# Layer 1: the bias folding moved to later steps one matrix at a time, and the last images' expert sums shared by three engines

## The chip, the cores and the metric

The kernel runs on one core of one Trainium2 chip. The metric is the device time of one launch in microseconds (us), as the median of several runs. Engines are named as in the profile: PE is TensorE (PEld its weight loads), DVE is VectorE, ACT is ScalarE, POOL is GpSimd, SP issues DMAs.

## What is computed

The input is `x` of shape (4, 32, 128, 128). Layer 0 is a spectral (FFT) convolution with attention between images; it writes its result `x1` to memory. Layer 1, where the change is, sees `x1` as four sequences of 4096 tokens with 128 channels. Cut to what matters here:

```python
# layer 1
t = x1 as tokens                                  # (4, 4096, 128)
# causal additive attention on normalised tokens
z = ln(t)
f, g = z @ W1[:128], z @ W1[128:]                 # 16 features each
score[i, j] = sum_a w2[a] * tanh(f[i, a] + g[j, a] + b1[a]) + b2
e = exp(score) * (j < i)
t = t + (e / (e.sum(-1) + 1e-10)) @ z
# mixture of 8 experts, the best two of each token
z = ln(t)
p, i = top_2(softmax(z @ router_w + router_b));  p = p / p.sum(-1)
t = t + sum_k p[k] * (z @ expert_w[i[k]] + expert_b[i[k]])
```

## The kernel before

A block of 128 tokens is called an image. Eight images make a chunk (16 chunks in all), and half a chunk, 512 query columns, is worked on at a time. **A unit** is one half of a chunk against one block of 128 keys; there are 528 units (`units`). The tanh sum is written with exponentials, so that it becomes matrix products: for each unit PE makes denominators `d` and numerators `n` (three groups each, L1869).

The order of the work in layer 1 is written out by hand, inside `tc.manual_schedule()`: a loop over `u`, in which each pass (a **step**) issues one stage of several units.

- PE: `d` of unit u together with `n` of unit u-1 (`products`, L1869).
- ACT: the logarithm of `d` of unit u into `r` (L1938), and then the exponential of minus that (L1950).
- DVE: `r = n * r` of unit u-1, in two instructions (L1943). POOL: two adds of the three groups into `e` (L1946, L1947).
- ACT: the exponential of `e` of unit u-2 (L1954); POOL multiplies the causal mask in on the diagonal (L1959).
- PE: the sum of `e` times the normalised keys of unit u-4 into `po` (`attend`, L1888); when a half is complete DVE copies it out (L1898).

Behind these each step issues **pieces** of the remaining work from queues: for the next chunk its load, its normalisation (statistics on DVE, L1504 and L1508; application on POOL, L1518), its transposes (L1533, L1534), its keys and queries (`as_keys`, `as_queries`: one matmul `pz`, one ACT exponential L1572 or L1587, and DMAs that copy 64 rows to the other half of the partitions); and for a chunk whose attention is complete the pieces of `finish`. A piece carries a kind and two costs, for DVE and POOL. The rule in the loop is: at most one piece with PE work in a step (`kind and pe`), at most 1.8 us of DVE cost and, beyond the first, 0.9 us of POOL cost. Whatever does not fit waits for the next step. A chunk's keys and queries are hurried when its first unit comes near (`hurry`).

All pieces with PE work use one PSUM bank, `"m"` (`misc`), until the loop is over; then four more banks join it. [...] a piece's matmul whose bank is still being read by DVE holds up the `d` and `n` of the next step.

`finish` adds the attention to the tokens `xc`, normalises (`x2`), transposes (`x2t`), computes router logits `pl` and the best two experts with DVE (`first`, `second`), the weights on ACT and POOL (`share`, `weights`, L1757), and then the experts (`experts`, L1770 and L1779): n products (image k, expert e) at a time, 2 to 4 by `share_of(u)`. PE writes them to one bank `px`, and DVE adds each, times its weight, to its image:

```python
nc.vector.scalar_tensor_tensor(
    xc[:, k], px[:, i], wgt[:, k, e : e + 1], xc[:, k], ALU.mult, ALU.add
)
```

After the loop, the remaining queues are emptied, and the last half chunk (four images, 32 products in 8 groups of 4) is finished alone with `last=True`; its store on SP is the last DMA of the kernel.

`biases` folds the router's and the experts' biases into the matrices `wr` (128x8) and `we` (128x1024), so that the kernel needs no separate addition: for each of three parts one matmul with `mean` (L1678), one DVE subtraction (L1679) and one DVE instruction that adds the bias row, read from `par` or `eb` (L1680). It is called at step u == 4, outside the rule for pieces, for all three parts. The tile `eb` lies in the buffer that `x2` uses from the first `finish` on.

Of the kernel before, what the change touches and what calls it, by code (L numbers as in the profile page):

```python
# [7 lines left out]
F32 = mybir.dt.float32  # L8
AF = mybir.ActivationFunctionType
ALU = mybir.AluOpType  # L10
# [3 lines left out]
P = 128  # L14
B, T, H, C = 4, 32, 128, 128
# [9 lines left out]
NE = 8  # L25
IC = 1024
NB = IC // P
QC = 512
# [4 lines left out]
B1, W2, RB = 11, 27, 43  # L33
# [1396 lines left out]
def layer1(tc, x1, w1t_in, signs, vec17, expert_w, expert_b, router_w, small_row, out):  # L1430


    nc = tc.nc
# [7 lines left out]
    def misc(name):  # L1441
        if not pools:
            return before.tile([P, 512], F32, name=name, tag="wide")
        banks.append(banks.pop(0))
        return ps.tile([P, 512], F32, name=name, tag=banks[-1])
# [14 lines left out]
    for s, dst in ((0, mq), (1, mk)):  # L1460
        pm = misc("pm")
# [21 lines left out]


    NONE, SOME, KEEPS, KEPT, EXPERTS, LATER = range(6)

    gap = (LATER, 0.0, 0.0, lambda: None)

# [142 lines left out]
    const, other_keys, work, small, ps = (p.__enter__() for p in pools)  # L1631
    banks.append("m")
    tc.keep_in_program_order(nc.scalar.preload_act_table_set("natural_log_exp_and_others"))
    par = const.tile([P, NSMALL], F32, name="par1")
    nc.sync.dma_start(out=par, in_=small_row.partition_broadcast(P))
    wr = const.tile([P, NE], F32, name="wr")
    nc.sync.dma_start(out=wr, in_=router_w)
    we = const.tile([P, NE, C], F32, name="we")
# [24 lines left out]
    mean = const.tile([P, P], F32, name="mean")  # L1663
    nc.vector.memset(mean, 1.0 / C)
    eb = work.tile([P, NE, C], F32, name="eb", tag="x2", bufs=1)
# [1 line left out]
        out=eb.rearrange("p e c -> p (e c)"),  # L1667
        in_=expert_b.rearrange("e c -> (e c)").partition_broadcast(P),
    )
    def biases():  # L1670
        for w, row in (
            (wr, par[:, RB : RB + NE]),
            (we[:, :4].rearrange("p e c -> p (e c)"), eb[:, :4].rearrange("p e c -> p (e c)")),
            (we[:, 4:].rearrange("p e c -> p (e c)"), eb[:, 4:].rearrange("p e c -> p (e c)")),
        ):
            n = w.shape[1]
            pm = misc("pm")[:, :n]
            nc.tensor.matmul(pm, mean, w, start=True, stop=True)  # L1678
            nc.vector.tensor_tensor(w, w, pm, ALU.subtract)  # L1679
            nc.vector.scalar_tensor_tensor(w, row, 1.0 / C, w, ALU.mult, ALU.add)  # L1680

    def finish(b, i0, nb, att, last=False):


        fe = [P, nb, NE]

        def over_e(t):
            return t.unsqueeze(2).to_broadcast(fe)

        def stat(tag):  # L1690
            return small.tile([P, NB], F32, name=tag, tag=tag)[:, :nb]

        xc = work.tile([P, NB, C], F32, name="xc", tag="xc", bufs=4)
        nc.sync.dma_start(out=xc[:, :nb], in_=x1[b, i0 : i0 + nb].rearrange("t w c -> w t c"))


        def attention(k0, n):
            pa = misc("pa")[:, : n * (C + 1)].rearrange("p (k c) -> p k c", c=C + 1)
            for k in range(n):
                q = (k0 + k) % QB * P  # L1700
                nc.tensor.matmul(  # L1701
                    pa[:, k], att[(k0 + k) // QB][:, q : q + P], centre, start=True, stop=True
                )
            rden = small.tile([P, 3, 1], F32, name="rden", tag="rden")[:, :n]
            nc.vector.tensor_scalar(rden, pa[:, :, C:], 1e-10, None, ALU.add)
            nc.vector.reciprocal(rden, rden)
            for k in range(n):
                nc.vector.scalar_tensor_tensor(
                    xc[:, k0 + k], pa[:, k, :C], rden[:, k], xc[:, k0 + k], ALU.mult, ALU.add
                )  # L1710

        x2 = work.tile([P, NB, C], F32, name="x2", tag="x2", bufs=1)
        x2t = work.tile([P, IC], F32, name="x2t", **(dict(tag="r", bufs=3) if last else dict(tag="x2t")))
        hot1, hot2, wgt = (
            small.tile([P, NB, NE], F32, name=n, tag=n, bufs=3)[:, :nb] for n in ("hot1", "hot2", "wgt")
        )
        top1, top2, vm, w1 = (stat(n) for n in ("top1", "top2", "vm", "w1"))

        at = {}

        def greatest(top, hot):
            pl, v = at["pl"], at["v"]
            nc.vector.tensor_reduce(top, pl, AX.X, ALU.max)
            nc.vector.tensor_tensor(v, pl, over_e(top), ALU.is_equal)
            nc.vector.tensor_tensor(v, v, rank.unsqueeze(1).to_broadcast(fe), ALU.mult)
            nc.vector.tensor_reduce(vm, v, AX.X, ALU.max)
            nc.vector.tensor_tensor(hot, v, over_e(vm), ALU.is_equal)

        def first():
            bank = misc("pl")
            at["pl"], at["v"] = (
                bank[:, i * nb * NE : (i + 1) * nb * NE].rearrange("p (k e) -> p k e", e=NE)
                for i in range(2)
            )
            pl = at["pl"]
            for k in range(nb):
                nc.tensor.matmul(pl[:, k], x2t[:, k * P : (k + 1) * P], wr, start=True, stop=True)  # L1739
            greatest(top1, hot1)  # L1740
            nc.vector.scalar_tensor_tensor(pl, hot1, -1e30, pl, ALU.mult, ALU.add)

        def second():
            greatest(top2, hot2)
            nc.gpsimd.tensor_tensor(top2, top2, top1, ALU.subtract)

        def share():

            nc.scalar.activation(top2, top2, AF.Exp)
            nc.scalar.activation(w1, top2, AF.Ln, bias=one)  # L1750
            nc.scalar.activation(w1, w1, AF.Exp, scale=-1.0)

        def weights():
            nc.gpsimd.tensor_tensor(top2, top2, w1, ALU.mult)
            nc.gpsimd.tensor_tensor(hot1, hot1, over_e(w1), ALU.mult)
            nc.gpsimd.tensor_tensor(hot2, hot2, over_e(top2), ALU.mult)
            nc.gpsimd.tensor_tensor(wgt, hot1, hot2, ALU.add)  # L1757

        products = [(k, e) for k in range(nb) for e in range(NE)]

        def experts(n):

            now = products[:n]
            del products[:n]
            px = misc("px").rearrange("p (e c) -> p e c", c=C)
            at_e = 0
            for k in sorted({k for k, _ in now}):
                own = [e for of, e in now if of == k]
                m = len(own)
                nc.tensor.matmul(  # L1770
                    px[:, at_e : at_e + m],
                    x2t[:, k * P : (k + 1) * P],
                    we[:, own[0] : own[0] + m],
                    start=True,
                    stop=True,
                )
                at_e += m
            for i, (k, e) in enumerate(now):
                nc.vector.scalar_tensor_tensor(  # L1779
                    xc[:, k], px[:, i], wgt[:, k, e : e + 1], xc[:, k], ALU.mult, ALU.add  # L1780
                )
            if not products:
                nc.sync.dma_start(
                    out=out[b, i0 : i0 + nb].rearrange("t w c -> w t c"), in_=xc[:, :nb]
                )
            return len(products)

        pieces = [(NONE, 0.0, 0.0, lambda: None), gap] * 2
        sums, after = norm_pieces(xc, x2, nb)
        step = 3 if nb == NB else 2  # L1790
        for k in range(0, nb, step):
            n = min(step, nb - k)
            pieces.append((SOME, 0.4 + 0.3 * n, 0.0, lambda k=k, n=n: attention(k, n)))
            pieces += sums[k // 2 : (k + n) // 2]
        pieces += after
        pieces += [
            (SOME, 0.7, 0.0, lambda h=h: transpose_half(x2, x2t, h)) for h in range(nb // 4)
        ]
        pieces += [(KEEPS, 1.4, 0.0, first), (KEPT, 1.2, 0.2, second), gap]
        pieces += [(NONE, 0.0, 0.0, share), gap, (NONE, 0.0, 1.1, weights), gap]  # L1800
        pieces.append((EXPERTS, nb * NE, 0.0, experts))
        return pieces

# [108 lines left out]
    def share_of(u):  # L1912

        queued = sum(ended, []) + todo
        left = sum(p[1] for p in queued if p[0] == EXPERTS) + sum(NE * p[2] for p in ending)
        others = sum(p[0] in (SOME, KEEPS) for p in queued) + NB * len(ending)
        until = min([f + 20 * (f < first_unit[-1]) for f in first_unit if f > u] + [len(units)])
        return min(max(-(-left // max(until - u - others, 1)), 2), 4)
# [12 lines left out]
    with tc.manual_schedule():  # L1931
        for u in range(len(units) + 4):
# [18 lines left out]
            if 0 <= u - 2 < len(units):  # L1951
                c, h, _, parts = units[u - 2]
                e = live[u - 2, "e"]
# [12 lines left out]
                elif is_last and h == 1:  # L1966
                    ending.append((*chunks[c], NB, [sums[c, h] for h in range(2)]))

            if u == 4:
                biases()  # L1970
            if unopened and not norm and u >= opens[unopened[0]]:
                norm_of = unopened.pop(0)
                norm, *opened[norm_of] = begin(norm_of)
# [12 lines left out]
            queues = sorted(ended, key=lambda p: len(p) <= 1)  # L1986
            queues = hurry + queues + [q for q in (todo, norm) if q not in hurry]
            pe, dve, pool = False, 0.0, 0.0
            n = share_of(u)
            for pieces in queues:  # L1990
                while pieces:
# [123 lines left out]
```

## Time and profile before

| what | value |
|---|---|
| median of 3 runs | 2872.17 us (2871.64 to 2875.78) |
| profiled execution, own time | 2870.23 us |
| profiled execution, span | 2868.6 us |
| granted TensorE clock, mean | 0.985 |
| busy share of the span | PE 95%, ACT 81%, DVE 76%, POOL 71% |
| layer 1's units | from 836.6 us to 2797.4 us of the span (first and last start of L1950) |
| work after the last unit | 2797.4 us to the end at 2868.6 us |

The profile is one execution. Busy time is what an engine executed; waiting for a semaphore is not busy. A row of the timeline gives the start, the duration of the (merged) instructions, the engine, the line, the operation with its output and inputs and shapes, the count, and in square brackets how long the engine was idle before it and what released it. L1950 is issued once for each unit, so the distance of two starts of L1950 is the time of a unit.

### The profile page before, as it was taken

The numbers are of one execution on the slowest core, as the hardware profiler recorded it, in microseconds if no ns is written. First come the engines' busy times: TensorE is split into PE (matmuls) and PEld (weight loads), VectorE is DVE, ScalarE is ACT, GpSimd is POOL, SyncE is SP. The second block draws the span as 40 slices with busy tenths as digits, with TensorE's granted clock in tenths as the row PEclk, the third lists the DMA queues.
The fourth block names the chain that finished last, engine by engine and source line by source line (L and its number), as shares of the span: only waits on it lengthen the run. The fifth ranks groups of instructions, "written<-read, shape, count | busy, mean of one in ns | idle before, by whom it ended". The sixth has DMA issues, their size and how long they took to land.

```text
span 2868.6 us, 52910 instructions
## 1 busy us (share of the span) xinstructions
PE 2720.7 (95%) x19638; PEld 1379.6 (48%) x19638; DVE 2175.5 (76%) x4830; ACT 2315.7 (81%) x3243; POOL 2035.3 (71%) x1804
## 2 busy tenths in 40 slices
PE   8898999988879999999999999999999999999996
PEld 5565664654644444445444444544444454444442
DVE  5888788778766677777787776778788677877777
ACT  3555466465459999999999999999999999999990
POOL 2706418137028998998998988898898888878872
PEclk9999999999989999999999999999999999999998
DMA  4403204114030101002101000110100010010000
GB/s 103 125 1 106 88 8 149 39 42 138 3 81 23 41 1 41 8 14 47 40 2 34 16 16 19 41 27 23 41 1 16 20 34 19 16 34 1 16 12 19
DMA packets 151153, 107.72 MB, mean 38 GB/s; under 512 B 36302, under 2 KB 140017, under 8 KB 150897
## 3 DMA queue, kind: packets, MB, share of 16 engines
q1 hardware_dynamic: 147633, 102.26, 13.5%
q8 instruction: 155, 2.54, 0.4%
q10 hardware_dynamic: 3264, 2.10, 0.3%
q14 instruction: 101, 0.83, 0.1%
HBM read 63.86 MB, written 19.50 MB: 29 GB/s over the span
## 4 chain that ended last, share of the span: by engine, by line
PE 60%; ACT 7%; DVE 5%; POOL 3%; issue 2%; DMA 0%; SPq 0%; DVEq 0%; POOLq 0%; ACTq 0%
PE d L1869 26%; PE po L1888 15%; PE px L1770 6%; PE n L1869 5%; ACT r L1938 3%; DVE r L1943 1%; ACT e L1954 1%; DVE xc L1779 1%; ACT r L1950 1%; PE pl L1739 1%; POOL e L1946 1%; PE pz L1571 1%; PE pa L1701 1%; PE pt L1533 1%; PE pz L1586 1%
## 5 line engine op out<-in xcount | busy, mean ns | idle before, releaser
L1943 DVE TENSOR_TENSOR r<-n,r 128x1024 f32<-128x1024 f32 (+1 forms) x1056 | 961.9, 953 | 457.3 <-PE n L1869 327.9
L1938 ACT ACTIVATE r<-d 128x1024 f32<-128x1024 f32 (+1 forms) x1056 | 793.6, 803 | 63.6 <-PE n L1869 51.4
L1946 POOL TENSOR_TENSOR e<-r 128x512 f32<-128x512 f32 x528 | 673.4, 1275 | 213.0 <-DVE r L1943 211.4
L1950 ACT ACTIVATE r<-r 128x1536 f32<-128x1536 f32 x528 | 783.6, 1484 | 16.8
L1947 POOL TENSOR_TENSOR e<-e,r 128x512 f32<-128x512 f32 x528 | 671.8, 1272 | 41.4
L1869 PE MATMUL d<-qe,ke 32*128 32x512 f32 (+3 forms) x2304 | 604.5, 601 | 16.9 <-ACT r L1938 12.8
L1869 PE MATMUL n<-qe,ke 32*128 32x512 f32 (+3 forms) x2304 | 604.6, 601 | 0.0
L1888 PE MATMUL po<-e,kx 128*128 128x512 f32 (+3 forms) x1152 | 594.4, 605 | 3.0 <-POOL e L1959 3.0
L1869 PE MATMUL n<-qf,kf 32*128 32x512 f32 (+3 forms) x2304 | 550.8, 553 | 0.0
L1869 PE MATMUL d<-qf,kf 32*128 32x512 f32 (+3 forms) x2304 | 549.1, 552 | 0.0
L1779 DVE SCALAR_TENSOR_TENSOR xc<-px,wgt,xc 128x128 f32<-128x128 f32 x1024 | 354.5, 349 | 34.9 <-PE px L1770 5.2
L1888 PEld LDWEIGHTS po<-e,kx 128*128 128x128 f32 x1152 | 175.4, 188 | 376.1 <-issue 297.6
L1954 ACT ACTIVATE e<-e 128x512 f32<-128x512 f32 x528 | 324.2, 614 | 14.7 <-POOL e L1947 14.7
L1869 PEld LDWEIGHTS d<-qe,ke 32*128 32x128 f32 x2304 | 176.5, 183 | 302.0 <-ACT r L1938 273.2
L1869 PEld LDWEIGHTS d<-qf,kf 32*128 32x128 f32 x2304 | 219.1, 185 | 164.4 <-issue 152.6
L1770 PE MATMUL px<-we,x2t 128*128 128x512 f32 (+3 forms) x644 | 271.0, 515 | 5.7 <-DVE xc L1779 2.0
L989 POOL TENSOR_TENSOR u<-xb,gb 128x858 f32<-128x858 f32 (+1 forms) x112 | 220.6, 2008 | 42.4 <-PE po L926 37.6
L1869 PEld LDWEIGHTS n<-qf,kf 32*128 32x128 f32 x2304 | 227.5, 185 | 24.8 <-issue 17.2
L1140 POOL TENSOR_TENSOR spec<-part,part 128x512 f32<-128x512 f32 x16 | 25.7, 1609 | 284.8 <-DVE gn_r_t L253 93.0
L993 DVE TENSOR_TENSOR u<-xw,gb 128x858 f32<-128x858 f32 (+1 forms) x208 | 215.6, 1105 | 6.7 <-ACT xw L980 3.1
L1770 PEld LDWEIGHTS px<-we,x2t 128*128 128x128 f32 x644 | 119.3, 193 | 140.4 <-issue 116.8
L1869 PEld LDWEIGHTS n<-qe,ke 32*128 32x128 f32 x2304 | 176.8, 183 | 10.9 <-DVE r L1943 1.5
(425 smaller groups left out, 3409.3 us busy)
## 6 DMA issues: line engine op xcount, KB each, us to landing
xb<-xd SPq DMA_DIRECT2D x128, 214.5 KB
xc<-x SPq DMA_DIRECT2D x29, 512.0 KB
x<-x SPq DMA_DIRECT2D x16, 512.0 KB
qf<-qe SPq DMA_DIRECT2D x64, 128.0 KB
out<-xc SPq DMA_DIRECT2D x15, 512.0 KB
x<-in_x SPq DMA_DIRECT2D x14, 512.0 KB
xb<-xd SPq DMA_DIRECT2D x32, 198.0 KB
kf<-ke SPq DMA_DIRECT2D x32, 128.0 KB
```

The source lines that it names most:

```text
L989: weighed = nc.gpsimd.tensor_tensor(u, xb, gk, ALU.mult)
L993: weighed_last = nc.vector.tensor_tensor(u, xw, gk, ALU.mult)
L1770: nc.tensor.matmul(px[:, at_e : at_e + m], x2t[:, k * P : (k + 1) * P], we[:, own[0] : own[0] + m], start=True, stop=True,)
L1779: nc.vector.scalar_tensor_tensor(xc[:, k], px[:, i], wgt[:, k, e : e + 1], xc[:, k], ALU.mult, ALU.add)
L1869: nc.tensor.matmul(o, k, q, start=turn == 0 or g > 0, stop=turn == 1 or g > 0)
L1888: nc.tensor.matmul(sums[c, h][:, q0 : q0 + c1 - c0], kx[:, jb], e[:, c0:c1], start=jb == 0, stop=is_last and q0 > 2 * P, skip_group_check= ...
L1938: nc.scalar.activation(r[:, g], d, AF.Ln, scale=1.0 / DSCALE)
L1943: nc.vector.tensor_tensor(r[:, g], part, r[:, g], ALU.mult)
L1946: nc.gpsimd.tensor_tensor(e, r[:, 1], r[:, 2], ALU.add)
L1947: nc.gpsimd.tensor_tensor(e, e, r[:, 0], ALU.add)
L1950: nc.scalar.activation(r, r, AF.Exp, scale=-1.0)
L1954: nc.scalar.activation(e, e, AF.Exp)
```

## The change

Three things are edited.

1. `biases()` at step 4 is gone. The three parts stand in a list, and each even step from u = 10 (`BIASES`) takes one: first `wr`, then `we[:, :4]` at u = 12, then `we[:, 4:]` at u = 14. Such a step counts as having its PE piece, and 1.4 us of DVE cost, so that the pieces that would have stood there move on.
2. In the last `finish` the products are reordered: four experts of one image, then the same four of the next image, so that groups of even and odd images alternate.
3. In the last `finish` the groups of odd images are no longer added by DVE: ACT copies each product from PSUM to a tile `scaled` times its weight, and POOL adds it to `xc`.

```diff
+    BIASES = 10
...
-    def biases():
-        for w, row in (
-            (wr, par[:, RB : RB + NE]),
-            (we[:, :4].rearrange("p e c -> p (e c)"), eb[:, :4].rearrange("p e c -> p (e c)")),
-            (we[:, 4:].rearrange("p e c -> p (e c)"), eb[:, 4:].rearrange("p e c -> p (e c)")),
-        ):
-            n = w.shape[1]
-            pm = misc("pm")[:, :n]
-            nc.tensor.matmul(pm, mean, w, start=True, stop=True)
-            nc.vector.tensor_tensor(w, w, pm, ALU.subtract)
-            nc.vector.scalar_tensor_tensor(w, row, 1.0 / C, w, ALU.mult, ALU.add)
+    def bias(w, row):
+
+        n = w.shape[1]
+        pm = misc("pm")[:, :n]
+        nc.tensor.matmul(pm, mean, w, start=True, stop=True)
+        nc.vector.tensor_tensor(w, w, pm, ALU.subtract)
+        nc.vector.scalar_tensor_tensor(w, row, 1.0 / C, w, ALU.mult, ALU.add)
+
+    biases = [
+        (we[:, 4:].rearrange("p e c -> p (e c)"), eb[:, 4:].rearrange("p e c -> p (e c)")),
+        (we[:, :4].rearrange("p e c -> p (e c)"), eb[:, :4].rearrange("p e c -> p (e c)")),
+        (wr, par[:, RB : RB + NE]),
+    ]
...
         products = [(k, e) for k in range(nb) for e in range(NE)]
+        if last:
+            products = [(k + i, e + j) for k in range(0, nb, 2) for e in (0, 4) for i in range(2) for j in range(4)]
...
+            if last and now[0][0] % 2:
+                scaled = work.tile([P, QC], F32, name="scaled", tag="e", bufs=5)
+                scaled = scaled.rearrange("p (e c) -> p e c", c=C)
+                for i, (k, e) in enumerate(now):
+                    nc.scalar.activation(scaled[:, i], px[:, i], AF.Copy, scale=wgt[:, k, e : e + 1])
+                    nc.gpsimd.tensor_tensor(xc[:, k], xc[:, k], scaled[:, i], ALU.add)
+                now = []
             for i, (k, e) in enumerate(now):
                 nc.vector.scalar_tensor_tensor(
...
-            if u == 4:
-                biases()
...
             pe, dve, pool = False, 0.0, 0.0
+            if biases and u >= BIASES and u % 2 == 0:
+                bias(*biases.pop())
+                pe, dve = True, 1.4
             n = share_of(u)
```

## The prediction

> **What bounds the kernel now.** I read the page's busy line first. It spreads its shares over two layers, so it does not tell what an edit in layer 1 is worth:
>
> ```profile
> PE 2720.7 (95%) x19638; PEld 1379.6 (48%) x19638; DVE 2175.5 (76%) x4830; ACT 2315.7 (81%) x3243; POOL 2035.3 (71%) x1804
> ```
>
> So I went to the timeline of layer 1 by ACT alone. L1950 runs once in a unit, and the distance of its starts is the unit's time:
>
> ```profile
> 851.01 1.48 ACT L1950 ACTIVATE r<-r 128x1536 f32<-128x1536 f32 x1
> 852.40 0.61 ACT L1954 ACTIVATE e<-e 128x512 f32<-128x512 f32 x1
> 857.36 0.69 ACT L1572 ACTIVATE ke<-pz,off 128x512 f32<-128x512 f32 x1 [4.35 <-PE pz L1571]
> 860.59 1.51 ACT L1938 ACTIVATE r<-d 128x1024 f32<-128x1024 f32 x2 [2.54 <-PE n L1869]
> 862.14 1.48 ACT L1950 ACTIVATE r<-r 128x1536 f32<-128x1536 f32 x1
> ...
> 866.15 1.48 ACT L1950 ACTIVATE r<-r 128x1536 f32<-128x1536 f32 x1
> ...
> 869.58 1.48 ACT L1950 ACTIVATE r<-r 128x1536 f32<-128x1536 f32 x1
> ...
> 873.01 1.48 ACT L1950 ACTIVATE r<-r 128x1536 f32<-128x1536 f32 x1
> ```
>
> The last two distances are 3.43 us with no idle time in brackets: ACT runs back to back and sets the pace. From 862.14 to 866.15 it is 4.01 us, because a key or query exponential (0.67 us) joins. One unit, from 851.01 to 862.14, takes **11.13 us**, and ACT sits idle 4.35 + 2.54 us in it. I took all 528 starts and sorted the units by the experts piece in the step before (median; units with a key or query exponential apart): no PE piece 3.43 us, two products 3.44, three 3.63, four 3.84. With three or four PE, not ACT, is the bound.
>
> The slow unit is where `biases()` stands. In the timeline of all engines:
>
> ```profile
> 850.76 1.27 POOL L1946 TENSOR_TENSOR e<-r 128x512 f32<-128x512 f32 x1
> 850.81 1.24 DVE L1680 SCALAR_TENSOR_TENSOR wr<-par,wr 128x8 f32<-128x8 f32 x1
> 850.83 1.12 PE L1678 MATMUL pm<-we,mean 128*128 128x512 f32 x2 [0.81 <-DVE wr L1679]
> 851.99 0.69 DVE L1679 TENSOR_TENSOR we<-we,pm 128x512 f32<-128x512 f32 x1
> 852.72 1.21 DVE L1680 SCALAR_TENSOR_TENSOR we<-eb,we 128x512 f32<-128x512 f32 x1
> 852.74 1.73 PE L1678 MATMUL pm<-we,mean 128*128 128x512 f32 x2 [0.78 <-DVE we L1679]
> 855.25 2.08 PE L1571 MATMUL pz<-xt,mk 128*128 128x512 f32 x2 [0.78 <-DVE we L1679]
> 857.25 1.22 PE L1869 MATMUL d<-qe,ke 32*128 32x512 f32 x2
> ```
>
> PE and DVE hand one bank to and fro: each `pm`, and then `pz`, waits for the subtraction before it. The matmuls grow longer meanwhile (`pm` 1.12 to 1.73 us).
>
> The end of the kernel, from the same view:
>
> ```profile
> 2843.51 22.03 SPq L1783 DMA_DIRECT2D out<-xc  x2
> 2852.62 0.25 POOL L1757 TENSOR_TENSOR wgt<-hot,hot 128x32 f32<-128x32 f32 x1
> 2852.91 12.22 DVE L1779 SCALAR_TENSOR_TENSOR xc<-px,wgt,xc 128x128 f32<-128x128 f32 x32 [1.44 <-POOL wgt L1757]
> 2857.60 1.10 PE L1770 MATMUL px<-we,x2t 128*128 128x512 f32 x2 [0.29 <-DVE xc L1779]
> ```
>
> The last 32 expert additions are one DVE chain of 12.22 us (0.382 each), ending at 2865.13. PE is done at 2858.7, ACT and POOL are idle, and only the store follows (to 2868.6).
>
> [...] the 128x8 L1680 took 1.24 us and ended at 852.05, when POOL's add (to 852.03) ended. [...] L1779 (one input in PSUM) took 317 to 353 ns in all 1024 cases. [...] The trace has 128x128 from PSUM with two pointers (L1405) at 478 and 0.37 back to back. [...] The trace's nearest row, L1959 at 128x128, took 0.45 to 0.47.
>
> **The change, part by part.**
>
> *Step 4.* Three matmuls and six DVE instructions leave. What stays is a unit with a key exponential, 4.01 us. Gain 11.13 - 4.01 = **7.1 us**. Nothing absorbs it: before and after it ACT runs back to back. Bounds 6.5 to 7.7 (the unit could fall to 3.43).
>
> *Steps 10, 12, 14.* The same instructions return singly. In each, the matmul waits for nothing: the bank was left a step ago. `wr`: two passes of 0.2 us beside 1.02 us of `po`; PE has room for about 0.5 us behind `po` before ACT waits (two products: 3.44). Cost 0. A `we` part has a 128x512 matmul, as four products have: 3.84 - 3.43 = 0.41 each, so 0.8. Then DVE: 0.69 + 0.69 us, the second with two SBUF inputs, next to a POOL that in these steps has two adds of 1.27 and an application of 0.8; it waits 0 to 1.27, say half. Queued behind it on DVE is the next L1943, which frees `n`'s banks for PE[...]. At step 12 DVE also has the 0.68 us `att` copy. With L1943's 1.82 DVE comes to about 1.82 + 0.68 + 2.0 = 4.5 us against 3.84. I take 0.4 us at step 12, 0.1 at step 14. Sum **+1.3**, bounds 0.5 and 3.5. No DMA moves.
>
> *The pieces that move on.* The order of instructions of the two programs, laid side by side by unit, shows that the first `finish` begins a step later, and that this runs on: in 235 of 528 units the pieces differ, up to unit 399; after it they are equal. Keys and queries stay 7 units ahead of their chunk in both (once 6 before), so no load comes late; SP's order of DMAs is a little permuted, each with the step of its piece. The pieces are as many, but packed otherwise: units with 4, 3, 2, 1 products go from 168, 52, 41, 2 to 185, 28, 42, 4 (912 products both). By the medians, +17 x 0.41 - 24 x 0.20 = **+2.2**. A linear fit of unit time on pieces gives +2.4, halves of the data 1.8 to 2.9. I take +2.1, bounds 0 and 5, since pieces can meet in combinations that the trace before has not.
>
> *The end.* DVE keeps 16 additions: 6.1 us, to 2859.0. ACT: [...] to about 2858.9, in step with PE's banks. POOL adds behind it: the first at 2852.9 + 0.4, then 16 of 0.46 plus up to 0.05 between dependent ones, about 7.8: to 2861.1. POOL now ends last, against 2865.13: **-4.0 us**. Bounds: 0.60 each, -2[...]. The store waits for DVE and POOL and costs the same 3.4 us.
>
> Sum: -7.1 + 1.3 + 2.1 - 4.0 = **-7.7 us**. On the profiled execution (span 2868.6, own time 2870.23) that is 2862.5; the median shown is 1.94 above that execution, so I forecast 2872.17 - 7.7 = **2864.5**. A measurement of this kernel can tell about 0.2% (5.7 us) from no change.
>
> **The rivals.** *The end is not shared.* If POOL's adds (two SBUF inputs) and DVE's additions exclude each other[...], the end is 6.1 + 7.4 + 0.4 = 13.9 us, +1.7 instead of -4.0: 2870.2. For it: the L1680 rows. Against: L1779's 353 ns at most, beside a busy POOL. Chance 0.08.
>
> *The stall moves with the biases.* If DVE, shut out by POOL, misses its slot in all three steps and each stalls PE by 1.8 us, they cost 5.4, not 1.3: 2868.6. For it: both 1.2 us rows. Against: one hand-over a step instead of three, and a free bank. Chance 0.12.
>
> *Slower.* The repacking of units 13 to 399 costs more than it seems: fours on a step where POOL applies a normalisation or DVE has statistics, with PE, DVE and POOL all at about 3.8. It decides from 9.8 us: 0.042 us more on each of 235 changed units. At 0.055, 13 us, the time is 2875. For it: fours do rise, and the fit's scatter is 0.13 us a unit. Against: fours with statistics were already there, at 3.7 to 3.84. Chance 0.05.
>
> **How the numbers follow.** The forecast has the remaining 0.75; its own spread from the bounds is about 2 us each way, with a tail above 2866.4. From it 0.68 and from luck in the others 0.05 give faster 0.73; same 0.22; slower 0.05. The range 2860.5 to 2869.5 takes in the centre of the moved stall, reaches close to that of the unshared end, and leaves the slower one out.
>
> **What would show it.** Unit 4 at about 4.0 us, ACT without the 4.35 us gap; `pm` rows alone at three places, units there at or under 4.5 us; L1680 again up to 1.2 us beside POOL. At the end POOL's 16 adds at 0.45 to 0.5 us, last to finish, about 8.2 us after `wgt`. The starts of L1950 from unit 149 to 400 some 2 us further apart than before. Wrong if the end still lasts over 11 us, if a bias step is over 5.5 us, or if units 16 to 399 lengthen by over 6 us.

## The result, and the profile after

The change takes 2864.49 us in the median of 9 runs (2862.19 to 2867.37); the kernel before takes 2872.17 us (2871.22 to 2875.78). The ratio is 0.9971 with a 95% interval of 0.9961 to 0.9981, so the change is faster by 7.7 us, between 5.5 and 11.2 us by the interval. The forecast was 2864.5. One execution of `end_20_12` further down took 8997.58 us, for a reason that is not known, and is left out of its ratio; all other executions of all kernels lie between 2856 and 2878 us.

The profiled execution of the change (span 2865.3 us, own time 2867.37) is the slowest of its nine, and only some 3 us shorter than that of before. So I compare stage by stage, by the starts of the instruction that runs once in a unit (L1950 before, L1962 now). ACT's timeline at unit 4:

```profile
855.76 1.48 ACT L1962 ACTIVATE r<-r 128x1536 f32<-128x1536 f32 x1
857.15 0.61 ACT L1966 ACTIVATE e<-e 128x512 f32<-128x512 f32 x1
857.67 0.67 ACT L1573 ACTIVATE ke<-pz,off 128x512 f32<-128x512 f32 x1
858.24 1.50 ACT L1950 ACTIVATE r<-d 128x1024 f32<-128x1024 f32 x2
859.77 1.48 ACT L1962 ACTIVATE r<-r 128x1536 f32<-128x1536 f32 x1
```

Unit 4 lasts 4.01 us, from 855.76 to 859.77, where it lasted 11.13. No row has idle time in brackets. A second thing is gone with the stall. The profile also records which share of PE's full clock was granted (PEclk, the third figure from the end of a row). Here is the old stall, and below it the three new bias steps in the change:

```profile
core 0: us, PE busy (x) PEld busy (x) DVE busy (x) ACT busy (x) POOL busy (x), PEclk, DMA share, GB/s
853.20:859.90 6.70, 5.92 (x16) 1.72 (x18) 2.11 (x3) 0.69 (x1) 2.87 (x3) 0.50 0.27 75
...
875.00:893.00 18.00, 17.17 (x98) 7.00 (x94) 12.32 (x17) 17.29 (x21) 17.26 (x19) 1.00 0.00 1
```

In all of these 6.7 us of the stall PE had half its clock. `pz` (128x512, x2) took 2.08 us in it, and 1.02 at 861.03, when the clock was 1.00 again. An estimate from these rows: at the full clock its 5.9 us of work would have taken about 3.0, so some 3 us of the 7.1 are a slower PE and not waiting. In the new steps the clock is full (1.00). The bias parts at steps 10 and 12, in the timeline of all engines (L1675 to L1677 are the lines of `bias`; step 14 looks like step 12):

```profile
876.61 0.28 PE L1675 MATMUL pm<-wr,mean 128*128 128x8 f32 x2
...
877.77 0.17 DVE L1677 SCALAR_TENSOR_TENSOR wr<-par,wr 128x8 f32<-128x8 f32 x1
...
883.81 1.02 PE L1675 MATMUL pm<-we,mean 128*128 128x512 f32 x2
...
885.02 0.68 DVE L1676 TENSOR_TENSOR we<-we,pm 128x512 f32<-128x512 f32 x1
...
885.73 1.00 DVE L1677 SCALAR_TENSOR_TENSOR we<-eb,we 128x512 f32<-128x512 f32 x1
...
886.17 1.23 POOL L1519 TENSOR_SCALAR kx<-xc,ln_r,ln_mr 128x128 f32<-128x128 f32 x1
```

No `pm` waits: none has a releaser in brackets. The 128x8 addition takes 0.17 us here, where it took 1.24 beside POOL's add. POOL was not idle here either: it was in the midst of a 1.66 us power of 128x8 elements (L1514, from 877.22) with two inputs in SBUF. So not every POOL instruction holds such a DVE instruction up. The 128x512 one takes 1.00 us instead of the 0.69 that it took at 855.23 in the stall, when POOL was idle, and POOL's application behind it 1.23 instead of the 0.79 that it takes at the same place in `slots_only`, a kernel below without the bias instructions. The end, from the same view:

```profile
2852.43 0.25 POOL L1760 TENSOR_TENSOR wgt<-hot,hot 128x32 f32<-128x32 f32 x1
2852.71 1.15 ACT L1787 ACTIVATE scaled<-px,wgt 128x128 f32<-128x128 f32 x4 [1.03 <-POOL wgt L1760]
...
2853.16 2.05 POOL L1788 TENSOR_TENSOR xc<-xc,scaled 128x128 f32<-128x128 f32 x4 [0.48 <-ACT scaled L1787]
...
2855.33 1.14 ACT L1787 ACTIVATE scaled<-px,wgt 128x128 f32<-128x128 f32 x4 [1.47 <-PE px L1775]
...
2855.84 6.18 POOL L1788 TENSOR_TENSOR xc<-xc,scaled 128x128 f32<-128x128 f32 x12 [0.63 <-ACT scaled L1787]
...
2857.90 1.51 DVE L1791 SCALAR_TENSOR_TENSOR xc<-px,wgt,xc 128x128 f32<-128x128 f32 x4 [0.21 <-PE px L1775]
```

Read from the bottom: DVE is done at 2859.4, POOL at 2862.0, 9.3 us after the weights, where DVE alone needed 12.3. POOL's 16 adds come to 8.23 us, and there is one gap of 0.63 us, which ACT, and through ACT the late `px` of PE, ends. In the single records an add lasts 0.45 us, and the next of the same image starts 0.53 us after it; only where POOL goes on from image 1 to image 3 does it start 0.42 us after it. DVE's four additions take 1.51 us beside POOL, as before.

### The profile page after: what moved, and what is told of

Its sections match the earlier page's. It is cut to its first block, busy times and chain, and to the rows that moved or that the text cites. A ratio compares the mean times of both kernels' runs of the same rounds, so it can differ in the third digit from the quotient of the medians.

```text
span 2865.3 us, 52957 instructions
## 1 busy us (share of the span) xinstructions
PE 2724.8 (95%) x19650; PEld 1384.8 (48%) x19650; DVE 2170.6 (76%) x4814; ACT 2319.7 (81%) x3259; POOL 2043.1 (71%) x1820
## 4 chain that ended last, share of the span: by engine, by line
PE 67%; ACT 8%; DVE 7%; POOL 6%; issue 3%; DMA 0%; POOLq 0%; DVEq 0%; ACTq 0%; SPq 0%
PE d L1881 26%; PE po L1900 15%; PE px L1775 7%; PE n L1881 5%; ACT r L1950 3%; PE po L926 2%; POOL u L989 2%; POOL e L1958 1%; DVE r L1955 1%; POOL e L1959 1%; PE pz L305 1%; ACT e L1966 1%; PE px L1123 1%; ACT r L1962 1%; PE pl L1742 1%
## 5 line engine op out<-in xcount | busy, mean ns | idle before, releaser
L1950 ACT ACTIVATE r<-d 128x1024 f32<-128x1024 f32 (+1 forms) x1056 | 793.9, 803 | 69.6 <-PE n L1881 57.2
L1962 ACT ACTIVATE r<-r 128x1536 f32<-128x1536 f32 x528 | 783.5, 1484 | 16.7
L1959 POOL TENSOR_TENSOR e<-e,r 128x512 f32<-128x512 f32 x528 | 671.8, 1272 | 41.4
L1881 PE MATMUL d<-qe,ke 32*128 32x512 f32 (+3 forms) x2304 | 605.3, 602 | 16.4 <-ACT r L1950 12.2
L1791 DVE SCALAR_TENSOR_TENSOR xc<-px,wgt,xc 128x128 f32<-128x128 f32 x1008 | 348.5, 349 | 34.4 <-PE px L1775 5.1
L1966 ACT ACTIVATE e<-e 128x512 f32<-128x512 f32 x528 | 324.3, 614 | 11.7 <-POOL e L1959 11.5
```

Source lines behind the costliest of these rows:

```text
L1791: nc.vector.scalar_tensor_tensor(xc[:, k], px[:, i], wgt[:, k, e : e + 1], xc[:, k], ALU.mult, ALU.add)
L1881: nc.tensor.matmul(o, k, q, start=turn == 0 or g > 0, stop=turn == 1 or g > 0)
L1950: nc.scalar.activation(r[:, g], d, AF.Ln, scale=1.0 / DSCALE)
L1959: nc.gpsimd.tensor_tensor(e, e, r[:, 0], ALU.add)
L1962: nc.scalar.activation(r, r, AF.Exp, scale=-1.0)
L1966: nc.scalar.activation(e, e, AF.Exp)
```

## The experiments

The starts of the units give a time for each stage that the scatter of whole runs (4 to 8 us from the fastest to the slowest of a kernel) hides. The table has, for the profiled execution of each kernel, by how many us each stage is longer than in the profile before: unit 4; units 9 to 24; 25 to 139; 140 to 399; and the end from the last unit's start. Units 400 to 527 differ by 0.03 us at most everywhere. The last two columns are the measured ratio and its interval.

| kernel | unit 4 | 9-24 | 25-139 | 140-399 | end | ratio | interval |
|---|---|---|---|---|---|---|---|
| the change | -7.1 | +0.1 | +0.1 | +2.0 | -3.1 | 0.9971 | 0.9961 to 0.9981 |
| change_again | -7.1 | +0.1 | +0.1 | +1.9 | -3.1 | 0.9972 | 0.9963 to 0.9982 |
| no_bias | -7.1 | 0.0 | -0.2 | -0.3 | -0.1 | 0.9978 | 0.9969 to 0.9988 |
| bias_9_10_11 | -7.1 | +0.5 | -0.6 | -0.5 | -0.1 | 0.9972 | 0.9962 to 0.9982 |
| bias_only | -7.1 | +0.2 | +0.3 | +2.0 | -0.1 | 0.9990 | 0.9984 to 0.9997 |
| bias_all_at_10 | -7.1 | +4.6 | -0.6 | -0.6 | -0.1 | 0.9985 | 0.9978 to 0.9991 |
| slots_only | -7.1 | -0.8 | -0.1 | +1.9 | -0.1 | 0.9983 | 0.9975 to 0.9991 |
| end_only | 0.0 | 0.0 | 0.0 | 0.0 | -3.6 | 0.9989 | 0.9983 to 0.9996 |
| end_20_12 | 0.0 | 0.0 | 0.0 | 0.0 | -4.2 | 0.9986 | 0.9979 to 0.9993 |
| change_warm | -7.1 | +0.2 | +0.3 | +2.0 | -3.3 | 0.9977 | 0.9968 to 0.9986 |
| placed_and_20_12 | -7.1 | +0.5 | -0.7 | -0.6 | -3.7 | 0.9960 | 0.9947 to 0.9972 |
| placed_20_12_warm | -7.1 | +0.5 | -0.7 | -0.6 | -5.7 | 0.9953 | 0.9940 to 0.9967 |

What is left out of the table is the start. The first unit begins between 836.6 and 841.3 us, though layer 0 is the same in all, and in three profiles (the change, bias_only, bias_all_at_10) the first unit is 1.3 to 1.8 us longer. For the change that is chance of the execution: `change_again`, the same program, begins 1.9 us earlier than it and has a normal first unit. For the others I take it to be the same, which is not shown. Because of it the sum of a kernel's stages and the difference of the medians disagree by up to 2.3 us (`slots_only`: 6.2 us faster by stages, 3.9 by medians). A stage difference of 1 or 2 us below is therefore read from one profile of each kernel, and the medians neither confirm nor deny it.

**no_bias.** Is the stall worth what it lasts?

```diff
-            if u == 4:
-                biases()
```

> The kernel before with the folding of the biases left out entirely (wr and we stay as loaded); all other instructions and their order as before. Theory A (at step 4 three matmuls, through one bank, hand PE and DVE to and fro, and nothing hides it): unit 4 falls from 11.1 to 4.0 us and the time by 7.1 us, to 2865.1. Theory B (much of the stall is later given back, since PE has slack): a fall of under 4 us.

Measured: 2864.59 us beside 2871.15; unit 4 is 4.01 us. Theory A holds: nothing gives the 7.1 us back. The later units even shrink by 0.5 us. It is mainly four units (76, 115, 231, 309) of 0.25 to 0.36 us each, here as well as in `bias_9_10_11` and `bias_all_at_10`, which keep the old pieces and have no stall at step 4; I did not find out why.

**bias_all_at_10.** Is it the place or the chain?

```diff
-            if u == 4:
+            if u == 10:
                 biases()
```

> The kernel before with its three bias parts together, but at step 10 instead of step 4; pieces as before. Theory A (the hand-over of the one bank is the cost, wherever it stands): step 10 takes 8 to 11 us instead of 3.4, the time is 2870 to 2873, about that of before. Rival (step 4 was slow since it stood between a query and a key piece that wait for each other, or for the late loads of par, we and eb): step 10 takes under 6 us, time 2865 to 2867.

Measured: 2866.92 us; step 10's unit takes 8.44 us instead of 3.43. Its timeline shows the same chain as before:

```profile
876.22 1.12 PE L1678 MATMUL pm<-we,mean 128*128 128x512 f32 x2 [0.90 <-DVE wr L1679]
...
878.10 1.62 DVE L1680 SCALAR_TENSOR_TENSOR we<-eb,we 128x512 f32<-128x512 f32 x1
878.12 2.02 PE L1678 MATMUL pm<-we,mean 128*128 128x512 f32 x2 [0.78 <-DVE we L1679]
...
880.07 1.22 PE L1869 MATMUL d<-qe,ke 32*128 32x512 f32 x2
...
882.84 1.51 ACT L1938 ACTIVATE r<-d 128x1024 f32<-128x1024 f32 x2 [4.89 <-PE n L1869]
```

The unit is as long as theory A expected, so the hand-over through one bank is a cost at step 10 too. The time of the whole run does not bear theory A out: 2866.92 lies in the range of the rival, since the stall is 5.0 us and not 7.1. Two things make it shorter. At step 10 no `pz` stands behind the third part, so that one wait of 0.78 us is missing. And PE was granted half its clock (0.50) for 3.4 us only (878.2 to 881.6), where it was 6.8 us before (853.1 to 860.0): `d` and `n` took 2.8 us to the start of L1938, and 3.3 before, where `pz` took 2.08 us too instead of the 1.02 of the next one (at 861.03).

**bias_9_10_11, bias_only, slots_only.** These three part the cost of the biases' instructions from that of the pieces that move on. The first has, in the change's loop, without its end,

```diff
-            if biases and u >= BIASES and u % 2 == 0:
-                bias(*biases.pop())
-                pe, dve = True, 1.4
+            if biases and u >= 9:
+                bias(*biases.pop())
```

The second is the change without its edits to the end; the third is the second with

```diff
-                bias(*biases.pop())
+                biases.pop()
```

> The kernel before, with the three bias parts one by one in steps 9, 10 and 11, which have no PE piece anyway, so that every piece stays in the step it had before. Theory A: the parts cost 0.1 to 1.3 us in all beside the units, so 2865.2 to 2866.4, within 1.3 us of the kernel without the folding. Rival (the stall moves with the biases, DVE being shut out by POOL): 5 us over the kernel without the folding, 2870.

> The change's bias edit alone (steps 10, 12, 14, each taking the step's PE piece), the end as before. Theory A with the repacking as predicted: -7.1 + 0.2 to 1.3 + 2.1, so 2867.4 to 2868.5, and some 2 us slower than the parts in steps 9, 10 and 11, all of it between units 140 and 400. Rival (repacking costs nothing, the difference was in the step of the biases): the same as steps 9, 10, 11 within 0.5 us.

> The change's bias edit without its instructions: the folding is left out, but steps 10, 12 and 14 still count as having their PE piece and 1.4 us of DVE, so that the pieces are packed as in the change; the end as before. Theory A: 2.1 us slower than the kernel before without the folding (2865.1), so 2867.2, the difference between units 140 and 400, where there are 17 more units of four products and 24 fewer of three. Rival (packing is neutral): 2865.

Measured: 2863.38, 2868.23 (both beside 2871.15) and 2867.98 (beside 2871.92). From the table, `slots_only` less `no_bias` is the packing alone: -0.83 in units 9 to 24, where pieces are only put off, +0.12, and +2.15 in units 140 to 399; together **+1.4 us**. `bias_only` less `slots_only` is the bias instructions in their steps: +0.97 + 0.46 + 0.15 = **+1.6 us**, of which only the first part lies at the steps themselves. In steps 9, 10 and 11 the same instructions cost 0.4 us against `no_bias` at the steps themselves; further on `no_bias` is longer (-0.4 and -0.2), for no reason that I found. The rivals fall: the stall does not move with the biases, and packing is not neutral. Of theory A the direction and the place stand, and the sizes do not all: the parts in steps 9, 10 and 11 are cheaper than expected, and the change's placing is 3.2 us slower than they by stages (4.9 by medians) instead of some 2, of which 2.5 lie between units 140 and 400.

**end_only and end_20_12.** The first is the kernel before with the change's edits to the end. The second, against the first, gives DVE 20 products and starts with POOL's:

```diff
-            products = [(k + i, e + j) for k in range(0, nb, 2) for e in (0, 4) for i in range(2) for j in range(4)]
+            products = [(k, e + j) for k, e in ((1, 0), (3, 0), (1, 4), (0, 0), (3, 4), (0, 4), (2, 0), (2, 4)) for j in range(4)]
...
-            if last and now[0][0] % 2:
+            if last and now[0] in ((1, 0), (1, 4), (3, 4)):
```

> The kernel before with the end of the change alone (last images' products reordered, odd images by ACT and POOL); biases at step 4 as before. From the profile of the change: from the weights to POOL's last add 9.3 us instead of 12.3, so 2869.2. Rival (POOL's adds and DVE's additions exclude each other): DVE's four additions longer than 1.51 us beside POOL, time 2872 or more.

> As the end alone, but DVE takes 20 of the last 32 products and ACT with POOL 12, and POOL's groups come first, third and fifth out of PE. If POOL's rate (0.51 us an add) and its wait for PE set the end: POOL ends about 7.0 us after the weights, DVE at 20 x 0.382 = 7.6 to 8.2 us; the time is 1.1 to 1.7 us below that of the end alone. Rival (the store's latency or something behind the adds sets the end): no gain over the end alone.

Measured: 2868.66 and 2867.75 beside 2871.92. In `end_only` the end is 3.6 us shorter, 0.6 more than in the change with the same instructions. The rows of POOL and DVE in its timeline:

```profile
2853.19 8.31 POOL L1785 TENSOR_TENSOR xc<-xc,scaled 128x128 f32<-128x128 f32 x16 [0.48 <-ACT scaled L1784]
...
2852.75 6.15 DVE L1788 SCALAR_TENSOR_TENSOR xc<-px,wgt,xc 128x128 f32<-128x128 f32 x16 [1.44 <-POOL wgt L1757]
```

There is one row for all 16 adds: here POOL never waits. PE's second group for it came 0.9 us sooner after the weights. PE's granted clock went back from 0.50 to 1.00 sooner, 6.1 us after the first logit matmul, where it was 7.8 us in the change, and the row of PE's 16 `px` matmuls lasts 9.25 us instead of 10.11. What sets that moment is not shown. No lock either: DVE's 16 additions take 6.15 us beside POOL, 0.384 each. So the rival of exclusion falls. `end_20_12` gains 0.5 us over `end_only`, less than half of the 1.1 us expected at the least, since DVE now sets the end and waits for `px` in its turn (0.40 and 0.21 us in its timeline).

**change_warm.** Four matmuls to keep PE busy ahead of the last transposes (`warm` is true in the last `finish` alone):

```diff
...
+        if warm:
+            pw = misc("pw")
+            for _ in range(4):
+                nc.tensor.matmul(pw, mean, we[:, :4].rearrange("p e c -> p (e c)"), start=True, stop=True)
         pt = misc("pt")
...
```

> The change with four more matmuls of 512 columns ahead of the last images' transposes, into a bank that nobody reads, to keep PE busy where it idles 6 us. Theory: PE's half clock is what keeps POOL waiting 0.63 us and stretches the logits from 1.0 to 1.9 us; with PE warm both shrink, and the end is 1.3 to 2 us earlier than in the change. Rival (PE's rate doesn't matter at the end, only POOL's): within 0.3 us of the change.

Measured: 2865.53, and an end 0.2 us shorter than the change's. The edit missed its aim. The matmuls were over at 2837.9, PE idled 1.7 us and then in gaps of 0.3 to 0.45 us between the transposes, its granted clock fell to 0.50 at 2840.3, and the logits took 1.88 us as before. So it is no test of what a full clock is worth. One thing can be read from it: four profiles have the change's end, and POOL's gap in them follows the moment at which the clock is full again. It is 0.63 us in the change (7.8 us after the first logit matmul), 0.59 in `change_again` (7.7), 0.36 here (7.3) and none in `end_only` (6.1).

**change_again, placed_and_20_12, placed_20_12_warm.** The best parts put together: biases in steps 9, 10, 11 and the end 20 to 12; the last one with seven matmuls ahead, and one of 256 columns after each transpose:

```diff
...
         for j in range(4):
             nc.tensor.transpose(pt[:, j * P : (j + 1) * P], src[:, 4 * h + j, :], ident)
+            if warm:
+                busy(1, 256)
...
```

> The change itself again, beside the next two on the same chip: about 7.7 us below the kernel before in the median; by stages of its trace unit 4 at 4.0 us, the units 9 to 400 together 2.0 to 2.2 us longer than before, and 68.0 to 67.5 us from the last unit to the end.

> The biases one by one in steps 9, 10 and 11, every piece in its old step, and the end shared 20 to 12. From the stages of the single runs: -7.1 at unit 4, -0.7 in the later units, -4.2 at the end, together 12 us below the kernel before and 4 us below the change. Rival (the stages do not add up, since a pace setter later takes the gain back): no more than 9 us below the kernel before.

> As placed_and_20_12, with seven matmuls of 512 columns ahead of the last transposes and one of 256 after each of the four, all into a bank that nobody reads, so that PE does not idle from about 2837 us to the logits. Theory (PE's half clock stretches the end): the eight logit matmuls take 1.0 instead of 1.9 us, the first four px groups come out in time, and the end is 0.9 to 1.5 us shorter. Rival (PE is not what the end waits for): the end within 0.3 us of placed_and_20_12.

Measured: 2863.76, 2859.47 and 2859.72 beside 2872.25. The stages add up: `placed_and_20_12` is 11.7 us faster than before by stages and 12.8 by medians, where 12 were expected; by medians both combinations are 4 us faster than the change. Whole runs, five of each, do not tell the two apart; their profiles do, which end 67.42 and 65.45 us after the last unit's start. The timeline of `placed_and_20_12`:

```profile
2840.85 0.47 PE L1534 MATMUL pt<-ident,x 128*128 128x128 f32 x1 [0.30 <-POOL x L1519]
...
2842.11 1.88 PE L1742 MATMUL pl<-wr,x2t 128*128 128x8 f32 x8 [0.78 <-DVE x2t L1535]
...
2850.25 1.51 DVE L1791 SCALAR_TENSOR_TENSOR xc<-px,wgt,xc 128x128 f32<-128x128 f32 x4 [0.81 <-PE px L1775]
```

and of `placed_20_12_warm`:

```profile
2840.38 0.27 PE L1541 MATMUL pt<-ident,x 128*128 128x128 f32 x1
...
2842.09 1.06 PE L1751 MATMUL pl<-wr,x2t 128*128 128x8 f32 x8 [0.35 <-DVE x2t L1544]
...
2847.10 7.57 DVE L1800 SCALAR_TENSOR_TENSOR xc<-px,wgt,xc 128x128 f32<-128x128 f32 x20 [1.43 <-POOL wgt L1769]
```

The same stretch of both, `placed_and_20_12` first, with PEclk again the third figure from the end:

```profile
2841.00:2849.20 8.20, 7.42 (x16) 4.02 (x17) 3.99 (x16) 1.85 (x7) 1.78 (x7) 0.50 0.00 0
...
2841.00:2849.20 8.20, 7.10 (x24) 3.54 (x24) 4.79 (x18) 2.81 (x12) 2.46 (x9) 1.00 0.00 0
```

With PE kept busy its clock stays full, the eight logit matmuls take 1.06 us instead of 1.88, a transpose 0.27 instead of 0.47, and DVE's 20 additions are one row without a wait. The end is 2.0 us shorter, more than expected: about 0.8 from the logits, 1.0 from DVE's waits (0.81 and 0.21), and the rest from the last transpose. That PE's rate matters to the end is shown, by one profile of each kernel. That it is also the reason of the 0.63 us gap in the change rests on the four profiles above; the change's own split was never run with a full clock.

## Why the prediction was right, point by point

- **Step 4.** Predicted -7.1, measured -7.1 (11.13 to 4.01). It read the sum from the unit's length, so it did not have to part waiting from clock. PE's waits there are 0.81, 0.78 and 0.78 us, and the granted clock was 0.50 from 853.1 to 860.0; what lowered it is not shown. It did not have the 0.5 us that later units gain in `no_bias`.
- **Steps 10, 12, 14.** Predicted +1.3; measured +1.6 by `bias_only` less `slots_only`. With the change's own profiles, whose units 9 to 399 are 0.4 us shorter than those of `bias_only`, it is +1.2. It put the part beyond PE's down to DVE waiting for POOL. The rows are longer on both sides: DVE's addition took 1.00 us, 0.69 with POOL idle, and POOL's application behind it 1.23 us, 0.79 without it. In the profile before, POOL's L1959 of 128x256 took 1.18 us at 853.33, where it began beside DVE's row of 1.21 us, and 0.72 at 850.08. What decides whether one holds up the other is not shown. Only 0.97 us lies where it put the whole, at the steps; and the 0.4 us between two kernels with the same loop (`bias_only` and the change) is not explained.
- **The pieces that move on.** Predicted +2.1 from counting fours and threes; the place was right (+2.15 in units 140 to 399), but the count had nothing for units 9 to 24, where pieces other than experts are put off and 0.8 us is saved. Net +1.4.
- **The end.** Predicted -4.0, measured -3.1. This is the mis-sized term, in two places. It took 7.8 us for POOL's adds: 0.46 of execution and at most 0.05 between two that depend on each other. They took 8.2: 0.453 of execution, and 0.08 between two of the same image. And it had PE's `px` in time, where PE's granted clock was 0.50 until 2854.7; POOL waited 0.63 us for it. ACT's copies were cheaper than the 0.37 us of L1405 (four in 1.14), which changed nothing.
- **The sum.** -7.7 predicted. By stages the change's two profiles give -7.1 + 2.2 - 3.1 = -8.0. The units came out 1.2 us better (a gain of 3.7 predicted, 4.9 measured), the end 0.9 worse; the two errors nearly cancel, and that the median was met so closely is luck to that extent.
- **The rivals.** The unshared end fell to `end_only`, and the moved stall to `bias_only` less `slots_only` (1.6 us, not 5.4) and to `bias_9_10_11`. The slower rival pointed to the right place, units 140 to 399, but at a fifth of its price.

## What to carry to other kernels

One serial chain of matmul and read-out through a single bank, issued in the midst of the stream of units, cost 7.1 us here, more than its waits on PE (0.81, 0.78 and 0.78 us), with PE's granted clock at 0.50 for 6.8 us; cut into links and put into steps that lack such work anyway, it cost 0.4 us at those steps. Where a list schedule is greedy, an added piece can cost about as much by pushing others (1.4 us here) as by itself (1.6): keep the schedule fixed and compare. And before dividing the last additions among engines, look at what feeds them: POOL waited 0.63 us for `px` here.

## What the runs showed that I had not expected

- PE's half clock (a granted share of 0.50) at the very end of the kernel was worth 2.0 us, two thirds of what sharing the additions brought in the change. Useless matmuls in its idle gaps bought it back when they filled the gaps up to the logits (`placed_20_12_warm`, 1.00 from 2841.0 to 2849.2), and not when they ended 1.7 us ahead of the transposes (`change_warm`, 0.50 from 2840.3).
- A unit late in the loop can depend on what happened hundreds of units before: four units became 0.25 to 0.36 us shorter each once the stall at step 4 was gone. The cause is open.
- The same layer 0 ended up to 4.7 us apart in different executions, about as much as each single edit here is worth. Stage by stage, two profiles of one program agreed within 0.1 us after the first unit.
- An addition that goes on with another image starts sooner than one that adds to the same image again. In the last images POOL's adds start 0.53 us apart within an image and 0.41 to 0.42 at the change of image, in all seven profiles with a shared end; DVE's start 0.386 us apart within an image and a group in the kernel before, and 0.268 at each of its three changes of image. Why is not shown. Giving each engine its images in turn was not tried. An estimate from these figures: 32 additions on DVE alone at 0.268 us would be 8.6 us instead of 12.2, if PE delivered `px` in time.
